# Attention and spectral-mixing kernel: the values of four heads from one product, and the order of the first loads at the joint of the layers

## The chip, the cores and the metric

One core of a Trainium2 chip runs the kernel. The metric is the device time of one execution in microseconds (us), as the median of several runs. The engines are named as the profile names them: PE (TensorE; its weight loads are PEld), DVE (VectorE), ACT (ScalarE), POOL (GpSimd) and SP (SyncE). PE writes its results to PSUM, a small memory of banks; everything else is in SBUF or in the chip's main memory.

## What is computed

The input `x` has 2 images of 128 channels and 64 x 64 points, which is 4096 tokens per image. Two layers follow each other:

```python
# layer 0
xn = group_norm(x)                                  # 32 groups
q, k, v = split(w_qkv @ xn + b_qkv)                 # 4 heads of 32 channels
q, k = rotary(q), rotary(k)
a = softmax(q.T @ k / sqrt(32)) @ v                 # per head, 4096 x 4096 scores
x = xn + w_proj @ a + b_proj
# layer 1, t = the tokens of x
y = layer_norm(t);  t = t + softmax(y @ y.T) @ y    # 4096 x 4096 scores per image
u = layer_norm(t);  t = t + sum_i(weights[i] * stu_i(u))   # 4 branches, weights from a hard softmax
```

`stu` is a convolution with 16 spectral filters, followed by matrices per filter, plus a short autoregressive term. It takes the second half of the kernel's time, and the change does not touch it.

## The kernel before, in words

**Tiles.** `P` = 128, `C` = 128 channels, `L` = 4096 tokens in `NT` = 32 tiles of 128 or `NQ` = 8 blocks of 512. `NH` = 4 heads of `CH` = 32 channels.

**Layer 0** (`layer0`) works through four units, one for each image `b` and pair of heads `pr`: (0,0), (0,1), (1,0), (1,1). A unit has 2 heads x 8 query blocks x 11 groups of up to `GT` = 3 key tiles. For a group PE makes three score products (128x512 each) into a PSUM tile of three banks (tag `st`, two of them), ACT takes the exponential of all three (L443), and two groups later PE weighs the values with them (three `acc` products, one bank). All `product`s (L190) are kept in the order in which the program writes them. Other instructions are put into each engine's queue by the scheduler of the framework, by priority and modelled times, unless the program fixes them with `keep_in_program_order`. [...]

While a unit runs, what the next one needs is made beside it, in small steps. `prepare` gives the steps: for each block of 512 tokens the query and key rows are projected (`projected`), turned (`rotate`, on DVE), and copied by DMA into stacked form (`stacks`). The values are projected by `values`, with a tile of 128 tokens as the stationary operand and the 64 columns of `wv` of the pair as the moving one, two tiles in a step, into the one PSUM bank of tag `ms` (`bank`). `split` then adds the bias `bv` and splits the float32 result into `NV` = 3 bfloat16 terms in `v`: one addition, three copies and two subtractions, all on DVE. A step is taken from the loop at three of the eleven groups (`BESIDE`).

For the first unit nothing runs beside: its steps are the startup. There a block's products go to the three banks of an `st` tile (`first`): two for queries and keys and their rotary partners, and one for the values of four token tiles. The copies of the split run on ACT and the subtractions on POOL.

When a query block is done, `close` copies `acc` to `accs` (L391). After two blocks, `divide` adds the three terms (L346, L348), sends the row of sums through DRAM and back by SP's queue (L345 to L352), and multiplies by the reciprocal (L355); `project` makes the output projection `po` for heads done (L365 adds it to the tokens).

`px` is a pool whose one tile of tag `a` (128 x 4096 float32) holds in turn the input of image 0, the input of image 1, and `hiT`, the first terms of layer 1.

**The joint.** During the last unit the normalised tokens of image 0 are split into a first term (`hi`, `hiT`, in SBUF) and a second one, which goes to DRAM (`lows`), since `loT` and `lo` have no room yet. When layer 0's pools are gone, `layers` (from L1079) allocates `lo` and loads the transform matrix `fw` (L796). The attention of layer 1 (`attend`) then calls `ready(i)` before each block of its first row: the first call loads second terms 0 and 1, each later one block i+1 (L1091, tile `low`, one buffer), and DVE copies them to `loT` and `lo` (L1092, L1093). The scores `y` (L911) are three products: hiT x hiT, hiT x loT, loT x hiT.

Beside `attend` run the rest of layer 0's division (`left`), the filters, and `matrices`: it takes `branch_weights` (L823 on: `z`, the sum of log weights and noise, its softmax `soft`, and the choice of a branch), and then mixes the branches' matrices on DVE, filter by filter.

Of the kernel before, what the change touches and what calls it, by code (L numbers as in the profile page):

```python
# [12 lines left out]
F32 = mybir.dt.float32  # L13
# [6 lines left out]
ALU = mybir.AluOpType  # L20
AX = mybir.AxisListType

P = 128
B, C, HH, WW = 2, 128, 64, 64
L = HH * WW
NH = 4
# [37 lines left out]
def conv_attn_hybrid(ctx: ExitStack, tc: tile.TileContext, io):  # L64
# [110 lines left out]
    def layer0(tok, px, last, side, beside_last):  # L175
# [3 lines left out]
        with ExitStack() as l0:  # L179
# [4 lines left out]
            def bank(name):  # L184
                return psum.tile([P, 512], F32, tag="ms", name=name, bufs=1)
# [3 lines left out]
            def product(*args, **kw):  # L189
                tc.keep_in_program_order(nc.tensor.matmul(*args, **kw))  # L190
# [13 lines left out]
            heads = p1.tile([P, 2], F32, name="heads")  # L204
            nc.scalar.dma_start(heads, io["heads"])

            def prepare(b, pr, xn):

# [1 line left out]
                qs = p2.tile([P, 2, L], F16, tag="qs", name=f"qs{u}")  # L212
                ks = p2.tile([P, 2, L], F16, tag="ks", name=f"ks{u}")
                v = p2.tile([P, NT, 2, NV * CH + 1], BF16, tag="v", name=f"v{u}")
                size = p2.tile([P, NQ], F32, tag="size", name=f"size{u}")

                first = (b, pr) == (0, 0)
# [32 lines left out]

                def values(at, n, pv):

                    pv = pv[:, : 2 * CH * n].rearrange("p (t g c) -> p t g c", g=2, c=CH)
                    for t in range(n):
                        product(
                            pv[:, t, :, :],
                            xn[:, bass.ts(at + t, P)],
                            wv[:, 2 * CH * pr : 2 * CH * pr + 2 * CH],
                            start=True,
                            stop=True,  # L260
                        )
                    return pv

                def split(at, n, pv):
# [24 lines left out]
                    return [p2.tile([P, 1024], F16, tag=f"term{n}", name=f"term{n}{u}_{i2}") for n in range(2)]  # L289

                def steps():
                    nc.gpsimd.memset(v[:, :, :, NV * CH :], 1.0)
                    for i in range(2):
                        table(i)
                    if not first:
                        yield
                    for i2 in range(NQ // 2):
                        term = terms(i2)
                        for h in range(2):
                            i = 2 * i2 + h  # L300
                            halves = [x[:, bass.ts(h, 512)] for x in term]
                            if first:
                                ps = psum.tile([P, GT, 512], F32, tag="st", name=f"first{i}")
                                pa, other = (projected(i, ps[:, n, :], w) for n, w in enumerate((wqk[:, pr, :], partner)))
                                pv = values(4 * i, 4, ps[:, 2, :])
                                rotate(i, pa, other, *halves)
                                if h:
                                    stacks(i2, term)
                                split(4 * i, 4, pv)
                            else:  # L310
                                rotate(i, projected(i, bank(f"pa{u}_{i}"), wqk[:, pr, :]), None, *halves)
                            yield
                        if not first:
                            stacks(i2, term)
                            for t in range(8 * i2, 8 * i2 + 8, 2):
                                split(t, 2, values(t, 2, bank(f"pv{u}_{t}")))
                                yield

                    top = p2.tile([P, 1], F32, tag="top", name=f"top{u}")
                    nc.vector.reduce_max(top, size, axis=AX.X)  # L320
                    keys = p2.tile([64, 1], F32, tag="keys", name=f"keys{u}")
                    nc.sync.dma_start(keys, top[64:, :])
                    yield
                    nc.vector.tensor_tensor(keys, keys, top[:64, :], ALU.mult)
                    yield
                    pk = bank(f"bound{u}")
                    nc.tensor.matmul(pk[0:1, 0:2], keys, heads[:64, :], start=True, stop=True)
                    nc.vector.tensor_copy(bound[:, b, 2 * pr : 2 * pr + 2], pk[0:1, 0:2])
                    yield

                return qs, ks, v, steps()

            ao = {}

            def divide(b, h, c, accs, wait):

                u = f"{b}_{h}_{c}"
                if h == 0:  # L340
                    ao[b, c] = (last if c == 3 else p1).tile([P, 1024], F32, tag=f"ao{c}", name=f"ao{b}_{c}", bufs=1)
                own = ao[b, c][CH * h : CH * h + CH, :]
                parts = [accs[CH * n : CH * n + CH, :] for n in range(NV)]
                rec = last.tile([CH, 1024 // CH], F32, tag="rec", name=f"rec{u}")
                nc.sync.dma_start(rec, accs[NV * CH :, :].rearrange("o (r s) -> o r s", r=CH))  # L345
                nc.vector.tensor_tensor(own, parts[0], parts[1], ALU.add)  # L346
                yield
                nc.vector.tensor_tensor(own, own, parts[2], ALU.add)  # L348
                nc.vector.reciprocal(rec, rec)
                back = dram.tile([CH, 1024 // CH], F32, tag="rec", name=f"back{u}", bufs=4)  # L350
                nc.sync.dma_start(back, rec)
                nc.sync.dma_start(parts[0], back.rearrange("r s -> (r s)").partition_broadcast(CH))  # L352
                for _ in range(wait):
                    yield
                nc.vector.tensor_tensor(own, own, parts[0], ALU.mult)  # L355
                yield
# [14 lines left out]
            xn = next(norm)  # L371
            for _ in norm:
                pass
            qs, ks, v, steps = prepare(0, 0, xn)
            beside = chain(steps, to_tokens(0, tok, xn, bank))
            pending = []
            accs = None
# [26 lines left out]
            for n, (b, pr) in enumerate(units):  # L404
                if n + 1 < len(units):
                    nxt = units[n + 1]
                    if nxt[1] == 0:
                        norm = group_norm(nxt[0], bank, p1, px)
                        xn = next(norm)
                        after = prepare(*nxt, xn)  # L410
                        beside = chain(beside, norm, after[3])
                    else:
                        after = prepare(*nxt, xn)
                        beside = chain(beside, after[3])
                else:
                    beside = beside_last(lambda n: p2.tile([P, NQ, 512], F32, tag=("qs", "ks")[n], name=f"stage{n}"))
# [35 lines left out]
                if n + 1 < len(units):  # L452
                    for _ in beside:
                        pass
                    qs, ks, v, _ = after
                    beside = to_tokens(nxt[0], tok, xn, bank) if nxt[1] == 0 else iter(())
            while pending:
                late()
# [230 lines left out]
    class LayerStats:  # L689
# [19 lines left out]
        def steps(self):  # L709
            for i in range(NQ):  # L710
                self.take(range(4 * i, 4 * i + 4))
                self.close(range(4 * i, 4 * i + 4))
                yield
            yield
# [19 lines left out]
    def layers(st, layer0):  # L734
# [58 lines left out]
        def transform(p):  # L793

            fw = p.tile([P, 4, NF], F32, name="fw", bufs=1)
            nc.sync.dma_start(fw, io["fw"])  # L796
            return fw
# [24 lines left out]
        def branch_weights(p):  # L822
# [4 lines left out]
            nc.gpsimd.dma_start(lg[:, 0, :], io["log_weights"].partition_broadcast(P))  # L827
            nc.gpsimd.dma_start(lg[:, 1, :], io["gumbel"].partition_broadcast(P))
            z = p.tile([P, NBR], F32, name="z")
            nc.vector.tensor_tensor(z, lg[:, 0, :], lg[:, 1, :], ALU.add)  # L830
            zm = p.tile([P, 1], F32, name="zm")
            nc.vector.tensor_reduce(zm, z, AX.X, ALU.max, negate=True)
            zs = p.tile([P, 1], F32, name="zs")
# [245 lines left out]
        with ExitStack() as l1:  # L1079
            p1 = pool(l1, "l1")  # L1080
            lo.append(p1.tile([P, L], F32R, name="lo"))
            fw = transform(p1)
            with ExitStack() as part:
                p = pool(part, "l1_a")
                gate = [0]

                def ready(i):
                    for n in range(2) if i == 0 else [i + 1]:
                        if n < NQ:
                            low = p.tile([P, 2, 512], F32, tag="low", name=f"low{n}")  # L1090
                            nc.sync.dma_start(low, lows[n].rearrange("n p c -> p n c"))  # L1091
                            nc.vector.tensor_copy(loT[0][:, bass.ts(n, 512)], low[:, 0])  # L1092
                            nc.vector.tensor_copy(lo[0][:, bass.ts(n, 512)], low[:, 1])  # L1093

                def closed(j):
                    gate[0] = j + 1

                y = [None]

                def stage(i, n):  # L1100
                    y[0] = p.tile([P, 512], F32, tag="y", name=f"y1_{i}")
                    return y[0]

                stats = LayerStats(p1, tok[1], "a1")
                steps = chain(left, stats.steps(), filters(p, fw), matrices(p), normalise(1, stats, stage, gate))
                attend(0, p1, steps, closed, ready)
# [345 lines left out]
```

## Time and profile before

| | |
|---|---|
| median of 3 runs | 2924.3 us (2923.44 to 2927.81) |
| profiled execution | 2924.81 us, of which the span is 2923.0 us |
| busy in the span | PE 2852.4, weight loads 1815.1, DVE 1689.9, ACT 1916.1, POOL 653.8 us |
| startup | to about 73 us; steady groups from about 80 us |
| units (0,0), (0,1), (1,0), (1,1) | to about 271, 549, 790 and 1026 us |
| joint | 1026 to about 1040 us |
| layer 1, attention of image 0 and 1 | to about 1400 and 1770 us |
| layer 1, spectral mixing | to 2923 us |

How to read it: the profile is one execution. The span is the time from its first to its last instruction; 1.8 us lie around it. Busy time of PE is modelled at its ends, so that a PE that is busy 98% of the time can still have room. What an engine waits for is inferred from semaphores. Line numbers are those of the kernel before.

### The profile page before, as it was taken

Reading aid. Unit: us, or ns where it says so; the run is one execution under the profiler, and the core shown is the slowest. Engines: PE = TensorE matmul, PEld = TensorE weight load, DVE = VectorE, ACT = ScalarE, POOL = GpSimd, SP = SyncE. Lnnn points to the kernel's source line nnn. Section 1 sums busy time; section 2 is a strip of 40 time slices with the busy share of each in tenths; the row PEclk is TensorE's granted clock in tenths of the full one; section 3 lists DMA queues with packets and bytes.
Section 4 is the critical chain, followed back from the end, with each engine's and each line's share of the span. In section 5 each row is a group of like instructions: output and inputs, shape, how many; then the busy total and the mean of one; then the engine's idle time right before and its main releaser. Section 6 shows DMA issues by size and latency. Waiting matters only on the chain. (4 is left out here: it accounts for less than half of the span.)

```text
span 2923.0 us, 40062 instructions
## 1 busy us (share of the span) xinstructions
PE 2852.4 (98%) x13872; PEld 1815.1 (62%) x13872; DVE 1689.9 (58%) x2916; ACT 1916.1 (66%) x2507; POOL 653.8 (22%) x1312
## 2 busy tenths in 40 slices
PE   5999999999999999999999999999999999999998
PEld 3555555555455577787777885666666666666665
DVE  5265562355243289877866677555555555555554
ACT  4999999999999956565555664444444444444442
POOL 3022120022000010000102003343444444444440
PEclk9999999999999999999999999999999999999999
DMA  4122120021001024100011002333333334333331
GB/s 137 33 63 77 48 66 16 5 78 48 6 33 35 4 83 128 57 1 1 26 39 40 8 26 68 97 89 93 92 85 82 81 77 115 82 85 84 82 82 54
DMA packets 166033, 175.91 MB, mean 60 GB/s; under 512 B 45264, under 2 KB 109536, under 8 KB 165824
## 3 DMA queue, kind: packets, MB, share of 16 engines
q1 hardware_dynamic: 122528, 137.05, 16.9%
q0 software_dynamic: 40304, 32.99, 5.4%
q10 hardware_dynamic: 2992, 3.22, 0.3%
q8 instruction: 115, 1.88, 0.3%
q14 instruction: 94, 0.77, 0.1%
HBM read 130.68 MB, written 25.49 MB: 53 GB/s over the span
## 5 line engine op out<-in xcount | busy, mean ns | idle before, releaser
L443 ACT ACTIVATE e<-s 128x1536 f16<-128x1536 f32 (+1 forms) x704 | 937.4, 1427 | 34.8 <-PE s L190 29.6
L1196 DVE TENSOR_TENSOR xl<-cv,xh 128x1024 fp32r<-128x1024 f32 x512 | 603.2, 1220 | 436.3 <-ACT xh L1195 349.0
L1195 ACT CAST xh<-cv 128x1024 fp32r<-128x1024 f32 x512 | 494.6, 1018 | 522.7 <-PE cv L1186 511.8
L1161 POOL DMA_DIRECT2D tokens_in<-rows x1024 | 490.5, 487 | 680.0 <-PE cv L1186 580.7
L190 PE MATMUL s<-qs,ks 128*128 128x512 f16 x2048 | 557.7, 379 | 11.8 <-ACT e L443 7.4
L190 PE MATMUL acc<-e,v 128*97 128x512 f16 x2048 | 557.1, 379 | 3.3 <-DVE accs L391 0.2
L1218 PE MATMUL m<-xh,loT 128*128 128x512 f32 x1024 | 409.5, 400 | 0.0
L1218 PE MATMUL m<-xh,hiT 128*128 128x512 f32 x1024 | 403.0, 394 | 0.0
L190 PEld LDWEIGHTS <-v 128*97 128x97 bf16 x2048 | 254.5, 124 | 214.3 <-issue 11.8
L190 PEld LDWEIGHTS <-ks 128*128 128x128 f16 x2048 | 200.5, 99 | 232.6 <-issue 46.9
L920 ACT ACTIVATE ey<-y,nshift 128x512 f32<-128x512 f32 x288 | 195.9, 689 | 201.4 <-PE y L911 179.2
L1186 PE MATMUL cv<-tables_in,tokens_in 32*128 32x512 f32 x2048 | 300.3, 646 | 1.8 <-DVE xl L1196 1.8
L1218 PE MATMUL m<-xl,hiT 128*128 128x512 f32 x1024 | 291.8, 417 | 1.2 <-DVE xl L1196 0.5
L1218 PEld LDWEIGHTS m<-xl,hiT 128*128 128x128 f32 x1024 | 178.6, 189 | 175.7 <-issue 104.7
L1218 PEld LDWEIGHTS m<-xh,loT 128*128 128x128 f32 x1024 | 192.5, 188 | 90.7 <-issue 47.8
L1218 PEld LDWEIGHTS m<-xh,hiT 128*128 128x128 f32 x1024 | 192.3, 188 | 42.2
L930 DVE TENSOR_TENSOR eT<-eT,eT 128x512 fp32r<-128x512 f32 x224 | 147.3, 684 | 112.9 <-ACT eT L929 112.0
L937 PE MATMUL oacc<-ep,hi 128*128 128x512 f32 x576 | 209.1, 411 | 1.2 <-DVE ep L969 1.2
L969 DVE TENSOR_TENSOR ep<-ey,ep 128x512 fp32r<-128x512 f32 x288 | 191.3, 684 | 7.6 <-PE oacc L937 1.4
L391 DVE COPY accs<-acc 97x512 f32<-97x512 f32 x64 | 44.2, 691 | 253.3 <-PE acc L190 253.3
L929 ACT ACTIVATE eT<-eT 128x512 fp32r<-128x512 f32 x224 | 133.1, 605 | 55.7 <-PE eT L927 55.5
L937 PE MATMUL oacc<-eT,hi 128*128 128x512 f32 x448 | 154.1, 405 | 2.2 <-DVE oT L975 1.2
(197 smaller groups left out, 3031.3 us busy)
## 6 DMA issues: line engine op xcount, KB each, us to landing
tables_in<-tables SPq DMA_DIRECT2D x1024, 64.0 KB, 3.3
tab<-in_rot SPq DMA_DIRECT2D x32, 512.0 KB, 4.1
tokens_in<-rows POOLq DMA_DIRECT2D x1024, 16.0 KB, 3.2
rows<-uh SPq DMA_DIRECT2D x64, 128.0 KB, 1.9
qs<-term POOLq DMA_DIRECT2D x112, 64.0 KB, 2.0
ks<-term POOLq DMA_DIRECT2D x96, 64.0 KB, 1.9
accs<-back SPq DMA_DIRECT2D x32, 128.0 KB, 2.3
lows<-stage SPq DMA_DIRECT2D x16, 256.0 KB, 2.0
```

Of the source, the lines that this page charges most:

```text
L190: tc.keep_in_program_order(nc.tensor.matmul(*args, **kw))
L443: nc.scalar.activation(e[:, own, :], ps[:, own, :], AF.Exp, scale=SCORE_SCALE)
L920: nc.scalar.activation(e[:, 2 * h + q, :], ps[:, q, :], AF.Exp, bias=nshift, accum_out=den[:, t, i : i + 1])
L929: nc.scalar.activation(eT[0], pt, AF.Copy, accum_out=den[:, 4 * i + u, j : j + 1])
L930: nc.vector.tensor_tensor(eT[1], pt, eT[0], ALU.subtract)
L937: nc.tensor.matmul(acc, a[0][:, own], c, start=(start and t == 0 and n == 0), stop=(stop and t == len(es) - 1 and n == 2),)
L969: nc.vector.tensor_tensor(es[t][1], e[:, t, :], es[t][0], ALU.subtract)
L1161: nc.gpsimd.dma_start(ut[part, :, :], rows[b][ci, row : row + BP, w0 : w0 + WC // 2, :])
L1186: nc.tensor.matmul(pu[:, h, :], ut[grp, w % 2, :], tt[grp, w % 2, :], start=True, stop=True)
L1195: nc.scalar.copy(hi, pu.rearrange("d h (c k) -> d k h c", k=NK))
L1196: nc.vector.tensor_tensor(seconds[n % 2][:, :, w, 64 * g2 : 64 * g2 + 64].rearrange("d k (h c) -> d k h c", h=2), pu.rearrange("d h (c k) ...
L1218: nc.tensor.matmul(acc, m, x, start=(s == 0 and w == 0 and i == 0), stop=(s == 1 and w == WC - 1 and i == len(products) - 1),)
```

## The change

There are three parts.

1. *Values.* For pair 0 of each image, `values` uses all 128 columns of `wv` for a token tile, so that the product holds all four heads. The first half goes through `split` as before. The second half, pair 1's, is copied without bias and without splitting, as float32, into a new tile `others` with tag `a` of the pool `px`: by ACT, four token tiles at a time, in the startup, and by DVE, two token tiles at a time, for image 1. `px`'s tile now holds in turn: input 0, `others` 0, input 1, `others` 1, `hiT`. For pair 1 no values are projected; `split` reads from `others` (`given`).
2. *Order.* Of the last division, the first addition (L346) and, in `branch_weights`, `z` (L830) are kept in the program's order.
3. *Joint.* The load and copies of second terms 0 are issued ahead of the load of `fw`, their first copy kept in the program's order; `ready(i)` loads block i+1 only.

```diff
-            def prepare(b, pr, xn):
+            def prepare(b, pr, xn, given=None):
...
+                others = []
...
-                    pv = pv[:, : 2 * CH * n].rearrange("p (t g c) -> p t g c", g=2, c=CH)
+                    pv = pv[:, : C * n].rearrange("p (t g c) -> p t g c", g=NH, c=CH)
                     for t in range(n):
-                        product(
-                            pv[:, t, :, :],
-                            xn[:, bass.ts(at + t, P)],
-                            wv[:, 2 * CH * pr : 2 * CH * pr + 2 * CH],
-                            start=True,
-                            stop=True,
-                        )
+                        product(pv[:, t, :, :], xn[:, bass.ts(at + t, P)], wv, start=True, stop=True)
...
                 def steps():
+                    if pr == 0:
+                        others.append(px.tile([P, NT, 2, CH], F32, tag="a", name=f"others{b}"))
...
-                                split(4 * i, 4, pv)
+                                nc.scalar.copy(others[0][:, 4 * i : 4 * i + 4, :, :], pv[:, :, 2:, :])
+                                split(4 * i, 4, pv[:, :, :2, :])
...
                             for t in range(8 * i2, 8 * i2 + 8, 2):
-                                split(t, 2, values(t, 2, bank(f"pv{u}_{t}")))
+                                if pr == 0:
+                                    pv = values(t, 2, bank(f"pv{u}_{t}"))
+                                    split(t, 2, pv[:, :, :2, :])
+                                    nc.vector.tensor_copy(others[0][:, t : t + 2, :, :], pv[:, :, 2:, :])
+                                else:
+                                    split(t, 2, given[0][:, t : t + 2, :, :])
                                 yield
...
-                nc.vector.tensor_tensor(own, parts[0], parts[1], ALU.add)
+                terms = nc.vector.tensor_tensor(own, parts[0], parts[1], ALU.add)
+                if wait > 1:
+                    tc.keep_in_program_order(terms)
...
-            nc.vector.tensor_tensor(z, lg[:, 0, :], lg[:, 1, :], ALU.add)
+            tc.keep_in_program_order(nc.vector.tensor_tensor(z, lg[:, 0, :], lg[:, 1, :], ALU.add))
...
-            fw = transform(p1)
             with ExitStack() as part:
                 p = pool(part, "l1_a")
                 gate = [0]
 
+                def second_parts(n):
+                    if n < NQ:
+                        low = p.tile([P, 2, 512], F32, tag="low", name=f"low{n}")
+                        nc.sync.dma_start(low, lows[n].rearrange("n p c -> p n c"))
+                        copy = nc.vector.tensor_copy(loT[0][:, bass.ts(n, 512)], low[:, 0])
+                        if n == 0:
+                            tc.keep_in_program_order(copy)
+                        nc.vector.tensor_copy(lo[0][:, bass.ts(n, 512)], low[:, 1])
+
                 def ready(i):
-                    for n in range(2) if i == 0 else [i + 1]:
-                        if n < NQ:
-                            low = p.tile([P, 2, 512], F32, tag="low", name=f"low{n}")
-                            nc.sync.dma_start(low, lows[n].rearrange("n p c -> p n c"))
-                            nc.vector.tensor_copy(loT[0][:, bass.ts(n, 512)], low[:, 0])
-                            nc.vector.tensor_copy(lo[0][:, bass.ts(n, 512)], low[:, 1])
+                    second_parts(i + 1)
+
+                second_parts(0)
+                fw = transform(p1)
```

The calls of `prepare` pass `others` of pair 0 on to pair 1 of the same image.

More of the change, by code (lines that the diff above doesn't have):

```diff
@@ L329, in steps @@
                     yield
-                return qs, ks, v, steps()
+                return qs, ks, v, steps(), others
             ao = {}
@@ L373, in layer0 @@
                 pass
-            qs, ks, v, steps = prepare(0, 0, xn)
+            qs, ks, v, steps, others = prepare(0, 0, xn)
             beside = chain(steps, to_tokens(0, tok, xn, bank))
@@ L412, in layer0 @@
                     else:
-                        after = prepare(*nxt, xn)
+                        after = prepare(*nxt, xn, others)
                         beside = chain(beside, after[3])
@@ L454, in layer0 @@
                         pass
-                    qs, ks, v, _ = after
+                    qs, ks, v, _, others = after
                     beside = to_tokens(nxt[0], tok, xn, bank) if nxt[1] == 0 else iter(())
```

## The prediction, made before the changed kernel was run

> **What bounds the kernel now.** I read the page first (busy shares, then the costliest groups), then busy time by stretch, then the waits of single stretches, and last the timeline of the few places that the change touches.
>
> ```profile
> PE 2852.4 (98%) x13872; PEld 1815.1 (62%) x13872; DVE 1689.9 (58%) x2916; ACT 1916.1 (66%) x2507; POOL 653.8 (22%) x1312
> L443 ACT ACTIVATE e<-s 128x1536 f16<-128x1536 f32 (+1 forms) x704 | 937.4, 1427 | 34.8 <-PE s L190 29.6
> L190 PE MATMUL s<-qs,ks 128*128 128x512 f16 x2048 | 557.7, 379 | 11.8 <-ACT e L443 7.4
> ```
>
> TensorE is busy 98% of the span, but its matmul ends are modelled, so that share does not prove that it sets the pace everywhere. In the attention of the first layer the exponentials (L443) stand back to back: 937 us of the some 950 us of those four units. Each engine waits a little for the other (29.6 us and 7.4 us). The stretches:
>
> ```profile
> 100.00:270.00 170.00, 169.99 (x821) 92.90 (x820) 89.26 (x197) 162.61 (x123) 33.59 (x68) 1.00 0.22 60
> 590.00:770.00 180.00, 179.37 (x845) 95.24 (x844) 90.41 (x203) 173.57 (x132) 31.60 (x64) 1.00 0.18 50
> 770.00:1026.00 256.00, 253.79 (x1190) 132.78 (x1189) 87.79 (x198) 252.53 (x192) 8.09 (x8) 1.00 0.06 21
> 1026.00:1040.00 14.00, 8.22 (x26) 5.62 (x25) 9.70 (x33) 5.18 (x13) 4.72 (x5) 0.76 0.54 153
> 1040.00:1120.00 80.00, 79.85 (x402) 63.76 (x401) 73.05 (x202) 48.34 (x137) 8.66 (x9) 1.00 0.27 92
> 1120.00:1200.00 80.00, 77.47 (x391) 62.14 (x389) 77.91 (x192) 45.60 (x129) 0.10 (x1) 1.00 0.40 119
> ```
>
> The columns are length, then busy time of PE, weight loads, DVE, ACT, POOL, then clock, DMA share, GB/s. In the first and third unit (rows one and two, where the next unit's values are projected beside) ACT is idle 7.4 and 6.4 us; in the last unit, where nothing is projected, only 3.5 us of 256 (1.4%). So projections on PE cost time there, but at most the difference: about 5.0 us of 170 and 3.9 us of 180. The waits of ACT in row one say the same:
>
> ```profile
> ACT e L443 <- PE s L190: 6.5, 17, 0.7
> ```
>
> At the joint of the layers PE stands still, and its clock falls (0.76):
>
> ```profile
> PE y L911 <- DVE loT L1092: 5.1, 1, 5.1
> 1033.04 0.79 PE L911 MATMUL y<-loT,hiT 128*128 128x512 f32 x1 [5.06 <-DVE loT L1092]
> 1033.63 0.63 PE L911 MATMUL y<-hiT,loT 128*128 128x512 f32 x1
> 1034.06 0.63 PE L911 MATMUL y<-hiT 128*128 128x512 f32 x1
> ```
>
> After the joint, rows five and six of the stretches have PE full and DVE at 91% and 97%: two engines without room.
>
> [...] after 5.06 us idle, matmuls start every 0.43 us until 1036.6, and about every 0.23 later. [...]
>
> **The values.** The timeline of two projection steps, one 64 columns wide (pv) and one 128 wide of the same type (po):
>
> ```profile
> 611.53 0.55 PE L190 MATMUL pv<-wv,xn 128*128 128x64 f32 x4
> 611.92 0.81 PE L190 MATMUL s<-qs,ks 128*128 128x512 f16 x3
> 527.89 0.61 PE L190 MATMUL po<-wp,ao 128*128 128x128 f32 x4
> 528.33 0.81 PE L190 MATMUL s<-qs,ks 128*128 128x512 f16 x3
> ```
>
> Start to start, two 64-column products hold PE 0.39 us, two 128-column products 0.44 us.
> - Removed: the 32 products each for pair 1 of batch 0 (in the first unit) and of batch 1 (third unit): 16 steps x 0.39 = 6.2 us of PE in each. Only ACT's excess idle can be won, 5.0 and 3.9 us. DVE still works there for the rotary part, and the PE peaks of `pa` (0.86 us each) stay: I take 3.6 us for the first unit and 3.4 us for the third, bounds 2 to 5 and 2 to 4.
> - Added, second unit: 16 x (0.44 - 0.39) = 0.8 us of PE beside the exponentials, and 16 DVE copies 128x128 out of PSUM. No row shows one. The nearest, the bias add of that shape out of PSUM (L270, 0.29 us), bounds it above[...]. 0.29 taken, 4.6 us in all; DVE is half idle, and the single bank comes free 0.3 us later: +0.5 taken, 0 to +1.5.
> - Added, startup: eight ACT copies 128x256 at about 0.41 us (the casts of v of that size), 3.3 us, ahead of the term copies on ACT, which is idle half the time before 73 us; the eight groups of four products grow by 0.1 us each.
> - Moved: the splits of pair 1 no longer wait for PE, so the schedule puts all 16 of batch 0 (six DVE instructions, 0.29 x 3 + 0.23 x 3 = 1.57 us, 25 us in all) early in DVE's queue, most of them between the rotary chains of the startup. There DVE waits now for other things:
>
> ```profile
> 46.51 1.41 DVE L236 SCALAR_TENSOR_TENSOR t<-first,bqk,tab 128x512 f32<-128x512 f32 x2 [3.84 <-DMA tab<-in_rot]
> 55.63 1.41 DVE L236 SCALAR_TENSOR_TENSOR t<-first,bqk,tab 128x512 f32<-128x512 f32 x2 [4.15 <-PE first L190]
> 71.93 1.41 DVE L236 SCALAR_TENSOR_TENSOR t<-first,bqk,tab 128x512 f32<-128x512 f32 x2 [5.49 <-PE first L190]
> ```
>
> By the changed kernel's order about three splits (4.7 us) stand in the first gap, 2.6 (4.1 us) in the second, 1.3 us between chains 5 and 6 where no gap is, and five (7.9 us) around 5.49 + 3.22 us of gaps. What overflows: 0.9 + 0 + 1.3 + 0, and some 0.3 us from early pieces: +2.5 us. Bounds +1 and +12: if the splits arrive after the gap (their source is copied by ACT late), the gap doesn't cover them and half of the 25 us is exposed.
> - Moved, too: the splits of batch 1's pair 1 go to the head of the third unit (from 549 us), some of them ahead of the division (L355) and of the copies of `acc` (L391) that PE waits for. DVE is busy there 16.7 of 41 us; 25 more fit in the 24 us left only if none comes at the wrong time. Following the order by hand, the copies at 564.4 and 580.9 come 2.6 and 4 us late; the two waiting score tiles hide about 0.9 us of each, and the slack of 0.09 us per group (1.38 of ACT against 1.30 of PE) gives some back: +2.0, bounds 0 and +5.
>
> **The joint.** Loading the first second terms ahead of `fw` lets their transfer (issue to landing 2.0 us) be over before PE comes. The copy to loT0 stands behind the copy of accs (1027.55, 0.69 us): PE goes on at about 1028.8 instead of 1033.04, with 0.8 us of idle: -4.3. The clock then has no reason to fall: some eight matmuls at 0.43 instead of 0.23: -1.6 (0 to -3). `rec` and `phi` on SP's queue move behind one more load, 0.4 us, which the division hides. In exchange the branch weights (z to coef, 20-odd small DVE instructions, about 4.8 us) go from this idle time to about 1072 to 1100 us, where DVE is 91% busy and PE full. Its room there (7 us) takes a part; the rest delays the `matrices` chain, at whose end, 1196 to 1202 us, PE already waits 3.4 us on DVE: +1.8, bounds 0 and +4.5.
>
> **Sum.** +2.5 - 3.6 + 0.5 + 2.0 - 3.4 - 4.3 - 1.6 + 1.8 = -6.1 us. Against the profiled execution (2924.8 us; its span 2923.0 and 1.8 around it) that is 2918.7; that execution stands 0.5 above the median of the runs, 2924.3, so the forecast is 2918.2. About 0.2% (5.8 us) is what a measurement can tell from none.
>
> **Rivals.**
> 1. *All of it counts.* The projections are PE's excess, as the 29.6 us of ACT waiting for PE say, and the hoisted splits fall into gaps: +1 - 5.0 + 0 + 0 - 3.9 - 4.3 - 3 + 0 = -15, 2909. Against it: 11 small waits remain even in the last unit, and chains at the startup without a gap.
> 2. *Given back.* The exponentials set the pace (1.38 against 1.30 us) and DVE sets it after the joint: +2.5 - 2 + 0.8 + 3 - 2 - 4.3 - 0.5 + 4.5 = +2, 2926. For it: DVE at 97% in the sixth stretch. Against it: ACT's idle in the first unit is twice that of the last.
> 3. *Slower: DVE's queue.* The hoisted splits are queued ahead of rotary chains, divisions and copies of acc. If their source comes late, or two chains' waits overlap, idle time doesn't cover them: startup +12, third unit +5, with -7 from the units and -4.1 from the joint: +6.4 with 0.5 for the wider products, 2931. It decides once the exposed part of the 50 us of splits is over about 16 us instead of my 4.5. For it: the splits read `others`, and ACT's copies of it come after the products. Against it: 13.3 us of DVE waits lie in just these places.
>
> **How the numbers follow.** Forecast 0.42, rival 1 0.15, rival 2 0.25, rival 3 0.18. Of the forecast's own range (2912 to 2923) some 0.6 is below the bound of 2918.5, and rival 2 crosses the upper bound in 1 of 6; so faster 0.25 + 0.15 = 0.40, same 0.17 + 0.21 = 0.38, slower 0.18 + 0.04 = 0.22. For 8 in 10 the range goes from rival 1 to just short of rival 3: 2909 to 2930; the forecast's own is 2912 to 2923.
>
> **What would show it.** Right: 64 pv products fewer; ACT idle in the first and third unit nearer 4 us; no wait of PE on loT over 1 us and a clock near 1 at the joint; the first exponentials of the steady stretch (79.8 us now) 2 to 3 us later. Wrong: longer waits of PE on accs at the start of the third unit, the steady stretch beginning over 5 us later, or waits of PE on DVE (ep, loT, eT) between 1080 and 1200 us that exceed what the joint won.

## The result

The changed kernel is slower: 2928.40 us (median of 20 runs, 2927.44 to 2931.27) against 2924.76 us (median of 20, 2922.84 to 2927.81); the ratio is 1.0014, 95% interval 1.0008 to 1.0020. The forecast was 2918.2, with 2909 to 2930 as the range: the time is inside it, the sign is not that of the forecast.

The page of the changed kernel shows what the change does (lines shift by 3 to 12): PE has 128 instructions and 7 us less.

```profile
PE 2845.4 (97%) x13744; PEld 1798.4 (61%) x13744; DVE 1691.5 (58%) x2932; ACT 1916.7 (65%) x2515; POOL 651.7 (22%) x1312
...
L449 ACT ACTIVATE e<-s 128x1536 f16<-128x1536 f32 (+1 forms) x704 | 936.2, 1435 | 35.6 <-PE s L190 31.2
...
L190 PE MATMUL s<-qs,ks 128*128 128x512 f16 x2048 | 557.9, 379 | 17.7 <-ACT e L449 8.7
```

There are 128 fewer because each of the 64 products that are gone counts two matmul records (`pv` x4 for the two of a step in the prediction's timeline). But PE stands idle longer ahead of the scores: 17.7 us instead of 11.8. Busy time by stretch, columns as in the prediction:

```profile
100.00:270.00 170.00, 169.30 (x775) 86.84 (x774) 68.60 (x110) 164.63 (x125) 33.45 (x68) 1.00 0.21 57
549.00:590.00 41.00, 36.92 (x191) 21.34 (x189) 34.81 (x113) 35.67 (x27) 0.41 (x1) 1.00 0.01 4
590.00:770.00 180.00, 178.47 (x796) 89.09 (x795) 69.67 (x110) 173.98 (x132) 31.29 (x64) 1.00 0.19 52
1026.00:1040.00 14.00, 11.29 (x50) 6.55 (x47) 3.62 (x10) 9.63 (x15) 4.99 (x5) 1.00 0.38 105
1040.00:1120.00 80.00, 79.39 (x399) 63.37 (x400) 74.68 (x218) 47.85 (x137) 8.65 (x9) 1.00 0.28 93
1120.00:1200.00 80.00, 76.14 (x376) 60.04 (x374) 75.59 (x184) 45.23 (x126) 0.00 (x0) 1.00 0.39 117
```

The second stretch, at the head of the third unit, was before:

```profile
549.00:590.00 41.00, 41.00 (x215) 24.07 (x213) 16.68 (x23) 38.79 (x29) 0.27 (x1) 1.00 0.06 17
```

In the first stretch 20 us of DVE work are gone (89.26 before) and ACT is idle 5.4 us instead of 7.4: the gain that was wanted. In the second, DVE has become busy (34.81 us instead of 16.68) and PE has lost 4 us. At the joint (fourth) the granted clock is 1.00 instead of 0.76, and PE is busy 11.29 us instead of 8.22.

To see where time is lost, I took events that every execution has: the first and certain later copies of `accs` (layer 0), the first exponential of layer 1 (L920), the 14th sum `oT` (at 1211.96 us before; DVE is busy 160.42 of the 172 us from 1040 us to there), and the end. Each entry is how much a stretch between two such events got longer than before, in us, from one profiled execution each. (The first unit ends with the 16th copy, at 304.0 us, not at 271 as the table of before has it.)

| stretch, from to in the kernel before | forecast | changed |
|---|---|---|
| startup, to 90.4 | +2.5 | +6.1 |
| first unit, to 304.0 | -3.6 | -3.0 |
| second, to 548.8 | +0.5 | +0.2 |
| head of the third, to 580.9 | +2.0 | +4.9 |
| its rest and the last, to 1027.6 | -3.4 | -3.1 |
| joint, to 1035.6 | -5.9 | -5.5 |
| full DVE, to 1212.0 | +1.8 | +5.1 |
| to the end, 2923.0 | 0 | -1.4 |
| sum | -6.1 | +3.3 |

All gains came at about the forecast size. Three losses came out 2.9 to 3.6 us larger than forecast each, 9.8 together. The stretch to the end differs between -1.5 and +0.3 over the executions of this study, though none changes the code there; it is not explained here. Some of the first stretch varies in the same way: the first rotary chain, ahead of which only one block's products are changed, starts between 26.20 and 28.11 us in them.

**Startup.** DVE's timeline. Split instructions of pair 1 (`left`, `v`) now stand between the rotary chains:

```profile
45.25 1.03 DVE L271 TENSOR_TENSOR left<-left,v 128x128 f32<-128x128 f32 x1
...
46.90 0.57 DVE L269 CAST v<-left 128x128 bf16<-128x128 f32 x1
...
50.07 1.40 DVE L238 SCALAR_TENSOR_TENSOR t<-first,bqk,tab 128x512 f32<-128x512 f32 x2
...
58.90 1.40 DVE L238 SCALAR_TENSOR_TENSOR t<-first,bqk,tab 128x512 f32<-128x512 f32 x2
...
77.73 1.40 DVE L238 SCALAR_TENSOR_TENSOR t<-first,bqk,tab 128x512 f32<-128x512 f32 x2
```

The three chains that the prediction showed started at 46.51, 55.63 and 71.93; none has a wait in brackets now, as DVE is busy without a gap. The first two lines show another thing: these instructions, a subtraction and a cast, take 0.29 and 0.23 us elsewhere.

**Head of the third unit.** The waits of PE from 545 to 600 us (total, times, longest; before there was none):

```profile
PE acc L190 <- DVE accs L397: 2.1, 2, 1.6
PE po L190 <- DVE ao L361: 2.0, 1, 2.0
```

DVE's timeline around the two instructions that PE waits for:

```profile
562.53 0.23 DVE L269 CAST v<-left 128x128 bf16<-128x128 f32 x1
562.79 1.22 DVE L361 TENSOR_TENSOR ao<-ao,accs 32x1024 f32<-32x1024 f32 x1
...
570.62 0.29 DVE L266 TENSOR_TENSOR left<-others,bv 128x128 f32<-128x128 f32 x1
570.83 0.68 DVE L397 COPY accs<-acc 97x512 f32<-97x512 f32 x1
```

From 552.2 to 571.4 DVE has no gap. Before, DVE had stood idle ahead of that copy of `accs`, and the copy came as soon as PE had the result:

```profile
564.40 0.69 DVE L391 COPY accs<-acc 97x512 f32<-97x512 f32 x1 [2.76 <-PE acc L190]
```

Counted from the copy at 548.83 (552.17 in the changed kernel), it now comes 3.1 us later, behind splits, and the next one, at 580.85, comes 4.9 us later.

**Joint.** PE waits 0.67 us for `loT` instead of 5.06. Then DVE stops at the reciprocal of the last division, whose row is still on its way, and the casts `ep` that PE needs stand behind it. ACT had their source, the first `ey`, ready by 1036.02 us, but DVE ran nothing ahead of the reciprocal, and the first cast began 0.27 us after it:

```profile
1033.79 0.50 PE L917 MATMUL y<-loT,hiT 128*128 128x512 f32 x1 [0.67 <-DVE loT L1096]
...
1037.07 0.34 DVE L355 RECIPROCAL rec<-rec 32x32 f32<-32x32 f32 x1 [3.00 <-DMA rec<-accs]
1037.34 0.35 DVE L974 CAST ep<-ey 128x512 fp32r<-128x512 f32 x1
...
1037.75 0.50 PE L943 MATMUL oacc<-ep,hi 128*128 128x512 f32 x1 [1.37 <-DVE ep L974]
```

### The profile page after: what moved, and what is told of

Same layout as the page of the kernel before. It is cut to its first block, busy times and chain, and to the rows that moved or that the text cites. A ratio compares the mean times of both kernels' runs of the same rounds, so it can differ in the third digit from the quotient of the medians.

```text
span 2926.3 us, 39807 instructions
## 1 busy us (share of the span) xinstructions
PE 2845.4 (97%) x13744; PEld 1798.4 (61%) x13744; DVE 1691.5 (58%) x2932; ACT 1916.7 (65%) x2515; POOL 651.7 (22%) x1312
## 5 line engine op out<-in xcount | busy, mean ns | idle before, releaser
L190 PE MATMUL s<-qs,ks 128*128 128x512 f16 x2048 | 557.9, 379 | 17.7 <-ACT e L449 8.7
```

## The experiments

The theory after this comparison: *queue order on DVE*. Splits and branch weights that now stand early in DVE's queue, or where DVE is full, cost more than PE's saving. The rivals: the wide products themselves cost it; or the two parts hurt each other. All times are medians, and the ratios are against the kernel before on the same chip. It took 2923.75 us on the chip of e1 to e4, 2925.20 on that of e5 to e8 and 2925.27 on that of e9 to e12, so times of different chips are compared by their ratios. The losses and gains of single stretches come from one profiled execution each.

### e1_pinned: the splits kept at their steps

```diff
-                    nc.vector.tensor_tensor(left, pv, bvb.unsqueeze(1).to_broadcast([P, n, 2, CH]), ALU.add)
+                    add = nc.vector.tensor_tensor(left, pv, bvb.unsqueeze(1).to_broadcast([P, n, 2, CH]), ALU.add)
+                    if pr:
+                        tc.keep_in_program_order(add)
```

> The changed kernel, but the first addition of each of pair 1's splits is kept in the program's order on DVE, so that the splits stay at their steps beside the units. Theory (DVE's queue): the loss at the startup and at the head of the third unit comes from the splits that stand ahead of rotary chains, divisions and copies of acc. Then the 17th block of layer 0 (first copy of accs) comes 0.5 to 1.5 us later than before instead of 6.1, the third unit's head loses under 1 us instead of 4.9, the first and third unit keep most of their 3 us each, and the whole is about 9 us below the changed kernel, 2919. Rival (wider products and the copies of the second half cost it): the first copy of accs still comes 5 to 6 us late, and the time stays within 2 us of 2928.

Measured: 2922.09 us, ratio 0.9995 (0.9986 to 1.0003), which can't be told from the kernel before. The order of DVE's queue is worth 5 to 6 us (by the medians +3.6 has become -1.7, the profiled spans differ by 6.1): the startup loses 3.0 instead of 6.1, the head of the third unit 1.2 instead of 4.9. The gains stay (-2.8, and -2.9 in the third unit's rest). But both theories missed the size at the startup: 3.0 remain. One reason is in the timeline of ACT and DVE:

```profile
49.31 1.45 ACT L451 ACTIVATE e<-s 128x1536 f16<-128x1536 f32 x1 [1.23 <-PE s L190]
...
50.66 0.37 ACT L309 COPY others<-first 128x256 f32<-128x256 f32 x1
...
51.13 0.42 DVE L266 TENSOR_TENSOR left<-first,bv 128x256 f32<-128x256 f32 x1 [2.19 <-ACT others L309]
```

and in the waits of DVE from 27 to 82 us:

```profile
DVE left L266 <- ACT others L309: 4.0, 4, 2.2
```

The copy of the second half (ACT) and the bias addition (DVE) read the same PSUM bank. The addition waits for the copy, four times and 4.0 us in all, and the copy stands behind an exponential. The bank, and with it one of the two score tiles, comes free at 51.5 us; in the kernel before the addition was at 47.84.

A second thing happens there. In the kernel before, the granted clock is 0.50 in each us from 44 to 50, with PE in a wait of 4.32 us until 46.97, and 1.00 again from 51; in e1 it is low for longer. The stretch from 42 to 58 us of the kernel before, of e1, of e2 (described next, whose startup is that of before) and of e11 (whose startup is that of e1):

```profile
42.00:58.00 16.00, 11.07 (x42) 5.49 (x41) 6.78 (x12) 8.16 (x11) 4.08 (x8) 0.79 0.67 170
42.00:58.00 16.00, 9.43 (x31) 4.42 (x31) 5.52 (x9) 9.46 (x15) 4.64 (x8) 0.68 0.64 169
42.00:58.00 16.00, 11.83 (x41) 5.95 (x41) 6.51 (x11) 8.24 (x11) 3.94 (x7) 0.68 0.63 165
42.00:58.00 16.00, 10.67 (x28) 4.65 (x28) 5.32 (x9) 8.83 (x13) 4.63 (x8) 0.57 0.62 165
```

Counted from the first rotary chain to the first copy of `accs`, e1 needs 3.1 us more than before, e2 0.6 and e11 4.1. A clock as low as e1's thus goes with 0.6 us where the code is that of before, and a still lower one with 1.0 us more than in e1, where the code is e1's.

### e2_joint and e3_values: one part each

e2 is the kernel before with parts 2 and 3 of the change: of the diff above, all from `terms` on. e3 is the other half: all ahead of `terms`.

> The kernel before with the joint's part of the change alone (second terms 0 ahead of fw, z and the last division's first addition kept in order). Theory (given back): from the last copy of accs to the first exponential of layer 1 5.5 us are won, and about 4.5 of them lost again by 1212 us, where DVE is full: 2923 to 2924.5. Rival (the give-back in the changed kernel comes from its other half, by shifted loads): 2919 to 2920.

> The changed kernel with the joint left as it was before: the values' part alone. Theory: +6.1 at the startup, -3.0 in the first unit, +0.2 in the second, +4.9 at the head of the third, -3.1 after it, and the joint as before: 5.1 us above the kernel before, 2930. Rival (the two parts hurt each other): 2925 to 2926.

Measured: e2 2921.73, ratio 0.9994 (0.9986 to 1.0002); e3 2929.14, ratio 1.0017 (1.0011 to 1.0024). The parts add within their intervals: -0.0006 and +0.0017 against +0.0014 for both. So the values' part made the kernel slower. Of the joint's part at most some 2 us are left, not clear of noise: e2 wins 5.5 us at the joint and loses 2.3 by 1212 us (why less than the changed kernel's 5.1, with the same code there, stays open). e2 lies between its theory and its rival; the rival of e3 falls.

### e4_z_free: the branch weights without their fixed order

```diff
-            tc.keep_in_program_order(nc.vector.tensor_tensor(z, lg[:, 0, :], lg[:, 1, :], ALU.add))
+            nc.vector.tensor_tensor(z, lg[:, 0, :], lg[:, 1, :], ALU.add)
```

> The changed kernel without the order on z: the schedule then puts the branch weights ahead of the last copy of accs on DVE. Theory: they wait there for the load of the log weights, which POOL issues only at the end of layer 0, so that the first exponential of layer 1 comes 2 to 5 us later than in the changed kernel; but the stretch up to 1212 us gives back 3 to 4.6 us less, and the time is 2926 to 2930. Rival (DVE is full there for another reason): the late start is kept, 2931 to 2933.

Measured: 2928.08, ratio 1.0014 (1.0007 to 1.0020). As the theory has it: the joint wins only 1.6 us instead of 5.5, and only 0.2 are lost by 1212 us instead of 5.1. Where the weights stand moves the loss, and does not remove it.

### e5_bias: one addition for four heads

Like e1, but DVE adds the bias of all four heads at once, from PSUM into `others`, and nothing else reads the bank.

```diff
+                def biased(at, n, pv):
+                    both = others[0][:, at : at + n, :, :]
+                    bvb = bv.rearrange("p (g c) -> p g c", g=NH)
+                    nc.vector.tensor_tensor(both, pv, bvb.unsqueeze(1).to_broadcast([P, n, NH, CH]), ALU.add)
+                    return both
...
-                                nc.scalar.copy(others[0][:, 4 * i : 4 * i + 4, :, :], pv[:, :, 2:, :])
-                                split(4 * i, 4, pv[:, :, :2, :])
+                                split(4 * i, 4, biased(4 * i, 4, pv)[:, :, :2, :])
```

> Like e1_pinned, but the bias of all four heads is added by one DVE instruction from PSUM into others (now four heads wide), and the splits of both pairs take their terms from there; the copies of the second half on ACT and DVE and the separate additions are gone. Theory (one bank, two readers): in e1_pinned the 3.0 us that are still lost at the startup come from DVE's addition waiting for ACT's copy of the same PSUM bank, which stands behind exponentials; then the first copy of accs comes at most 1 us later than before, and the time is 2919 to 2920.5. Rival (the wider products on PE cost it): 2.5 to 3 us remain, 2921.5 to 2922.5.

Measured: 2920.59, ratio 0.9984 (0.9978 to 0.9991). The startup still loses 2.5 us, as the rival had it, but 0.9 of them are there already at the first rotary chain (28.11 us, 27.20 before). From that chain on e5 loses 1.6 us (and e8, with the same code, 1.5), where e1, e6 and e7 lose 2.5 to 3.1: the theory's reason was real, and its cure is half of one. The rotary chains in DVE's timeline say why:

```profile
28.11 1.41 DVE L238 SCALAR_TENSOR_TENSOR t<-first,bqk,tab 128x512 f32<-128x512 f32 x2 [3.38 <-PE first L190]
...
32.19 1.41 DVE L238 SCALAR_TENSOR_TENSOR t<-first,bqk,tab 128x512 f32<-128x512 f32 x2
...
36.26 1.41 DVE L238 SCALAR_TENSOR_TENSOR t<-first,bqk,tab 128x512 f32<-128x512 f32 x2
...
40.65 1.41 DVE L238 SCALAR_TENSOR_TENSOR t<-first,bqk,tab 128x512 f32<-128x512 f32 x2
```

The first three follow each other at 4.07 us, where before it was 3.81 (27.20, 31.00, 34.81): DVE sets the pace of the first four blocks, and an addition of 128x512 takes 0.27 us more than one of 128x256. A part of the bank wait became DVE time. Over four chains this makes 0.8 us; the clock (0.68 from 42 to 58 us, as in e2) goes with another 0.6. That leaves about 0.2 us for the rival, wider products on PE, by an estimate from these single executions; no run tests it alone.

### e6_early: the branch weights in the last unit

On e1: the loads of log weights, noise and sigma, and all from `z` to `coef`, are traced as five steps of the last unit's `beside_last`, in tiles of the pool `last`; `matrices` takes `wbr` and `coef` from there.

```diff
+        def choose(p):
+            kept = tc.keep_in_program_order
...
+            kept(nc.vector.tensor_tensor(z, lg[:, 0, :], lg[:, 1, :], ALU.add))
...
         def beside_last(stage):
             first_parts()
             stages = [stage(n) for n in range(2)]
+            yield from choose(last)
             stats = LayerStats(last, tok[0], "a0")
```

> Like e1_pinned, but the branch weights (z to coef) are computed in the last unit of layer 0, where DVE is a third busy, and no longer after the joint. Theory (DVE is full from 1040 to 1200 us): of the 4.0 us that are lost between the first exponential of layer 1 and 1212 us about 1.3 remain, and the time is 2.5 us lower, 2919 to 2920. Rival (the wait is for something else, the weights fit in between): at most 0.8 us are won, 2921 to 2922.

Measured: 2918.13, ratio 0.9976 (0.9965 to 0.9986). From the first exponential to 1212 us only 0.7 us are lost, where e1 loses 4.0. The longest of PE's waits from 1040 to 1210 us, first of e1 (5.3 us in all):

```profile
PE eT L935 <- DVE loT L778: 1.7, 1, 1.7
PE oacc L945 <- DVE ep L976: 1.0, 1, 1.0
PE oacc L945 <- DVE oT L983: 0.8, 1, 0.8
PE yT L774 <- DVE y L727: 0.7, 1, 0.7
```

and of e6 (3.9 us in all):

```profile
PE yT L774 <- DVE y L727: 1.7, 1, 1.7
PE eT L950 <- DVE loT L778: 1.4, 1, 1.4
PE oacc L960 <- DVE ep L992: 0.3, 1, 0.3
```

The small waits on DVE (`ep`, `oT`) are nearly gone, and the last unit got no longer. But e6 moved more than some 4.8 us of small DVE instructions: the three loads that the weights need, which POOL issued at the joint, went with them. The row of the last division, which SP issues at 1026.87 us in e1 and at 1027.17 in e6, is then back sooner. The reciprocal that waits for it, first of e1, then of e6:

```profile
1030.38 0.34 DVE L357 RECIPROCAL rec<-rec 32x32 f32<-32x32 f32 x1 [2.85 <-DMA rec<-accs]
1028.90 0.34 DVE L357 RECIPROCAL rec<-rec 32x32 f32<-32x32 f32 x1 [1.09 <-DMA rec<-accs]
```

In all eight kernels that load the weights at the joint the row takes 3.4 to 4.0 us, in e6, e8, e9 and e10 1.7 to 1.9. With it PE's wait for `ep` at the joint falls from 1.21 us in e1 to 0.16 in e6. So the branch weights and their loads together are worth 3.3 us in this pair of kernels (between e2 and e10, below, the same move is worth 1.6), and some 1.0 us of either is the late row and not DVE's fullness. In the last unit, where DVE is a third busy (87.79 of 256 us before), they cost nothing.

### e7_rec and e8_all: the reciprocal behind its addition

```diff
-                nc.vector.reciprocal(rec, rec)
+                turned = nc.vector.reciprocal(rec, rec)
+                if wait > 1:
+                    tc.keep_in_program_order(turned)
```

> Like e1_pinned, but the reciprocal of the last division is kept behind its second addition on DVE; in the changed kernel it stands ahead of the first casts ep of layer 1 and waits for its row to come back by DMA. Theory (a wait in DVE's order): PE's wait of 1.4 us for ep goes, and the first oT comes 1.2 us earlier; 2920.5 to 2921. Rival (DVE is full later, so nothing is kept): no change at 1212 us, 2922.

> e5_bias, e6_early and e7_rec together. Theory: their gains add, 2.5 + 2.7 + 1.2 us below e1_pinned, 2915 to 2916.5. Rival (two of them take the same wait away): 2918 to 2919.

Measured: e7 2922.72, ratio 0.9991 (0.9983 to 1.0000); e8, with e5 and e6, 2918.67, ratio 0.9976 (0.9967 to 0.9985). e7 wins nothing that could be told from e1, and in e8 the gains did not add: its rival holds, since e6 alone had already taken the wait for `ep` away. PE's wait for `ep` is gone in e7 (0.16 us), and the next thing is late in its place, terms 1:

```profile
1030.24 0.51 PE L921 MATMUL y<-hiT 128*128 128x512 f32 x1 [0.32 <-ACT ey L930]
...
1032.32 0.50 PE L921 MATMUL y<-loT,hiT 128*128 128x512 f32 x1 [1.07 <-DVE loT L1100]
...
1033.39 0.63 PE L921 MATMUL y<-loT,hiT 128*128 128x512 f32 x1
1033.81 0.63 PE L921 MATMUL y<-hiT,loT 128*128 128x512 f32 x1
```

In this execution PE slowed down too: for seven matmuls the next one starts 0.43 us later, as it did in the kernel before at a granted clock of 0.50, which is an estimated 1.4 us more than at 0.23. The load of terms 1 had been issued only when terms 0 had left the one buffer `low`.

### e9_one and e10_none: which wide products pay

e9 is e6 with wide products for image 1 alone; e10 has none (layer 0 as before, the joint's part, the weights early). Of e9:

```diff
+                wide = b == 1
...
-                    if pr == 0:
+                    if wide and pr == 0:
```

> Like e6_early, but only image 1 makes its values by the wide product; image 0 projects pair by pair as before. Theory (image 0's trade is null: the 2.2 to 3.0 us that the wide product costs in the startup, where nothing hides it, stand against 2.7 us won in the first unit): the first copy of accs is within 0.5 us of before, the first unit wins nothing, and the time is within 1 us of e6_early, 2917 to 2919. Rival (the startup's loss comes from elsewhere): the first copy stays over 1.5 us late and the first unit's gain is missing, 2920 to 2921.5.

> Like e6_early, but no wide products at all: the joint's part of the change with the branch weights moved to the last unit. Theory: layer 0 as before, 5.5 us won at the joint and 0.7 to 1.2 of them lost by 1212 us: 2920 to 2921, that is 2 to 3 us above e6_early, which is what image 1's wide products are worth once their splits are pinned. Rival (the values' part is worth nothing even then): 2917.5 to 2919.

Measured: e9 2918.17, ratio 0.9974 (0.9964 to 0.9985); e10 2919.73, ratio 0.9982 (0.9974 to 0.9990). Image 0's trade is null: without its wide product the startup is as before (-1.0 and -0.2) and the first unit wins nothing (0.0). Image 1's, with pinned splits, takes 2.8 us off the third unit in e9's profile and none in e10's; the two medians differ by 1.6 (the theory had 2 to 3), and their intervals overlap.

### e11_low_two and e12_both: terms 1 in a buffer of their own

```diff
-                        low = p.tile([P, 2, 512], F32, tag="low", name=f"low{n}")
+                        low = p.tile([P, 2, 512], F32, tag="raw" if n == 1 else "low", name=f"low{n}")
```

> Like e6_early, but second terms 1 have a buffer of their own (that of tag raw, not used yet), so that their load is issued ahead of fw too and needn't wait for the copy of terms 0. Theory (the next thing late at the joint is terms 1): PE's wait of 0.5 us on them and the gaps before it go, 1 to 1.5 us in all, 2916.5 to 2917.5. Rival (ep and the exponentials are late there as well): no change, 2918.

> e9_one and e11_low_two together. If both theories hold it is as fast as e11_low_two, 2916 to 2918; if the startup matters more than thought, lower.

Measured: e11 2916.69, ratio 0.9970 (0.9959 to 0.9981); e12, with e9, 2915.99, ratio 0.9967 (0.9955 to 0.9979). The steps from e6 to e11 and from e9 to e12 (0.0006 and 0.0007) lie within the intervals. But PE now runs on through the joint; e12's timeline:

```profile
1026.44 0.50 PE L939 MATMUL y<-loT,hiT 128*128 128x512 f32 x1 [0.65 <-DVE loT L1118]
...
1029.40 0.50 PE L939 MATMUL y<-hiT 128*128 128x512 f32 x1 [0.37 <-ACT ey L948]
1029.74 0.39 PE L939 MATMUL y<-loT,hiT 128*128 128x512 f32 x1
1029.97 0.39 PE L939 MATMUL y<-hiT,loT 128*128 128x512 f32 x1
```

From the first exponential to 1212 us it is 1.4 us shorter than before. e12 is the fastest kernel of the study, 9.3 us below the one before (2925.27 on the same chip).

## Why the prediction was wrong, step by step

- *Removed products, first and third unit (-3.6 and -3.4): right*, -3.0 and -3.1, with the cap by ACT's idle time. Rival 1 (all counts) falls.
- *Second unit (+0.5): right*, +0.2. The 16 copies out of PSUM, taken at 0.29 us, took 0.28 each.
- *Moved splits, startup (+2.5, bounds +1 and +12): right to 0.6 us.* Pinning them takes 3.1 of the measured 6.1 away. Each gap was set against the splits ahead of it at 1.57 us for two token tiles. 13 split instructions took longer than elsewhere, by 6.3 us in all, and each of the 13 overlaps a subtraction on POOL. The 25 us were some 31, so that the sum came near in part by luck. How much falls to this term and how much to the next depends on which is taken away first: in the changed kernel DVE is busy throughout, and no wait for ACT's copies shows there.
- *Added, startup (ACT copies and wider products): the step that failed outright.* It named "eight ACT copies 128x256 at about 0.41 us", called ACT "idle half the time", and put nothing into the sum. What it put at nothing is 2.0 to 3.3 us: by so much the startup of the six with pinned splits and a wide product for image 0 (e1, e5 to e8, e11) lies above the execution of before, while the four with the old startup (e2, e9, e10, e12) lie 0.2 to 1.0 below it. In e1 the copies read the bank that DVE reads, so their place in ACT's queue counts and not ACT's idle share (4.0 us of waits); without that second reader (e5, e8) the loss from the first chain on is 1.5 to 1.6 us instead of 2.5 to 3.1. What remains there is, by the estimate above, the wider addition on DVE and a longer time at half clock, a cost that the prediction looked for at the joint alone.
- *Moved splits, head of the third unit (+2.0, bounds 0 and +5): the term was mis-sized.* Measured +4.9, with the mechanism as described: L355 and two copies of `accs` late, the copies by 3.1 and 4.9 us where the order read by hand gave 2.6 and 4. The allowance for waiting score tiles and for slack, some 2 us, did not come: PE's waits for `ao` and for `accs` add up (2.0 + 2.1 us).
- *Joint (-4.3 and -1.6): right*, -5.5. That the clock would not fall was an inference from one stretch, 0.76 with a wait of 5.06 us; it was 1.00 with waits of up to 1.37 us. What brings it down was not shown. One figure in it is misread: 2.0 us from issue to landing is that of the store `lows<-stage`, and the load of `low` takes 3.4 to 5.2. It did not matter, because the load was issued as early as 1009.17 us.
- *Branch weights (+1.8, bounds 0 and +4.5): mis-sized.* The stretch lost 5.1, above the bound. Moving the weights and their loads away takes 3.3 of it back from e1 to e6, and 1.6 from e2 to e10. Some 1.0 of either is PE's wait for `ep` behind the reciprocal (1.37 us in the changed kernel), a wait that the prediction didn't see; e7, which takes that wait alone away, shortens the stretch by 0.3 only, in an execution where seven matmuls started 0.43 us apart. What makes up the rest of the 5.1 stays open. "Its room there (7 us) takes a part" read an average over 80 us; in the kernel before, the stretch from 1060 to 1080 had 0.3 us of room.

Rival 3, that the hoisted splits' exposed part decides, had the right mechanism and too high a price (17 us; about 8 were exposed, 3.1 and up to 4.9). (The 13.3 us of waits that it was weighed against are 13.5 by the three lines shown.) Rival 2, the gain given back after the joint, had the right place. They happened together, each in part, and the sum ended between them. What went wrong in method: of four costs with bounds from both sides I took values in the lower half of each, and three of them have a common cause, instructions that stand in DVE's queue ahead of others (for two of the three, pinning them in e1 took off 3.1 and 3.7 us); and one cost was named and given no number.

## What to carry to other kernels

An instruction that loses its input's wait loses its place, too: where a scheduler orders by readiness, see where it lands in the engine's queue, and pin it if others behind it have a deadline: here that was worth 5 to 6 us. A second reader of a PSUM bank can cost what stands ahead of it on *its* engine, and not its own duration: in e1 2.19 us of wait for a copy of 0.37. Small work should go into a stretch where its engine is a third busy, and its loads with it: here some 4.8 us of it, where DVE was full, cost 1.6 to 3.3.

## What the runs showed of the hardware

The round trip of the division's row through DRAM, from the issue of `back` to that of `accs` on SP's queue, takes 1.3 to 1.5 us in most of the 32 places of an execution. At some places it is longer in every execution (at the joint 1.7 to 6.5 us), and at others only now and then, with the same code there: at the head of the third unit 1.3 or 2.7 to 3.6. Before, and in e1:

```profile
553.02 0.30 SPq L351 DMA_DIRECT2D back<-rec  x1
554.34 0.30 SPq L352 DMA_DIRECT2D accs<-back  x1
```

```profile
553.41 0.30 SPq L359 DMA_DIRECT2D back<-rec  x1
556.46 0.30 SPq L360 DMA_DIRECT2D accs<-back  x1
```

At the head of the third unit a projection waits for it. Of the executions with pinned or no hoisted splits, those with a slow trip there (e1, e6, e8, e11: 3.1 to 3.6 us) lose 1.2 to 1.8 us in that stretch, and those with a fast one (e2, e5, e7, e9, e10, e12: 1.3 us) none. So e1's 1.2 us there goes with this, and not with its code. In the changed kernel the trip was slow too (2.97 us), but DVE worked without a gap, so that the splits alone account for the 4.9. Why the trip is slow at times stays open.

In the startup of the changed kernel, 13 of DVE's small split instructions took longer beside POOL's work: a cast of 0.23 us took up to 1.08, a subtraction of 0.29 up to 1.12. Each of the 13 began while POOL was at work (on a subtraction or, three times, on a DMA issue just ahead of one); seven others, which were already running when a subtraction of POOL began, kept their 0.2 to 0.3 us. No run took POOL's subtractions away, so the cause was not shown.

The time at half clock in the startup comes in steps: 6.8 us before, in the changed kernel and in e4, e9, e10 and e12, 10.2 in e1 to e3 and e5 to e8, and 13.7 in e11, worked out from the granted clock around 42 to 58 us, taking it as full or half (before, it reads 1.00 or 0.50 in all windows of 1 us from 42 to 58 but the two at the turns, 0.87 and 0.71). The difference is 3.4 us each time. The same startup code can get different steps: e1 and e11, or the changed kernel and e3.
